# Transposing softmax probabilities on VectorE with block transposes and DMA in place of TensorE, and staggering the two attention units

## The chip, the cores and the metric

The kernel runs on one core of one Trainium2 chip. The metric is device time in microseconds (us) of one execution. Besides the execution times there is one profiled execution, read through several views: the summary page, groups of instructions by shape, the timeline of an engine, waits, the chain of work that ended last, and busy time in stretches. Engines are named as the profile names them: PE (TensorE matmuls), PEld (its weight loads), DVE (VectorE), ACT (ScalarE), POOL (GpSimd) and SP (the queue that issues most DMAs).

## The reference

Everything is float32. The input x has 4 batches of 512 rows of 1024 numbers; there are 16 heads of 64.

```
xn = layernorm(x)
q, k, v = xn @ Wq, xn @ Wk, xn @ Wv            # per head; rotary on q and k
p = softmax(causal(q @ k.T) / 8)               # 512 x 512 per head, lower triangle
s = (p @ v) @ Wo
r = softmax(xn @ gate_w.T)                     # 8 experts
f = ((xn * (r @ in_scale)) @ sign(weight).T) * (r @ out_scale) + bias
out = x + s * silu(f)
```

The change concerns the line of `p` and the product `p @ v`.

## The kernel before

The attention part runs over 16 groups, four to a batch. A group gives two units (`u0`, `u1`), and a unit is a pair of heads: its tiles hold head 0 in partitions 0 to 63 and head 1 in partitions 64 to 127 for q and k, or one head after the other in the free dimension for the probabilities. Query rows go in four tiles `i` of 128; tile `i` needs key columns 0 to 128(i+1) only, so a unit has 10 blocks (j, i) of 128 x 128 on or below the diagonal for each head.

The work of a unit, in the order of the code:

- `scores` (L517): for each query tile, one matmul per head into a PSUM tile. Then DVE adds the mask on the diagonal block (L528) and takes the row maximum (L532), ACT takes the exponential and the row sum (L535), DVE the reciprocal of the sum (L543), and POOL scales the probabilities (L545). `scores_1`, `scores_3` and `scores_02` do this for query tile 1, for tile 3, and for tiles 2 and 0, each time for both units of the group.
- `transpose_p` (L583): `p @ v` needs the probabilities with keys in partitions. TensorE transposes the 20 blocks of a unit through an identity matrix, four to a PSUM bank, and ACT (L589, three banks of five) or DVE (L587, two of five) copies the bank to an SBUF tile `pT`.
- `values` (L599): eight matmuls of v with the transposed blocks into one bank; DVE copies it over v's tile (L608), and SP stores that to DRAM (`at_d`, L609) for the output projection.

[...] Four are `ring`, used in turn by all projections, transposes and values; `ps_sc` is two tiles of two banks each for the scores, used also by `in_scales` and `out_scales` of the last batch.

TensorE's order is the order of the code, written by hand. While group k is projected (q, k and v, by a Strassen scheme of seven products for each pair of unit tiles: L342 for q and k, L429 for v), the attention of group k-1 is laid between the projection matmuls. One such stretch is called a slot: 84 projection matmuls (`fill`), spread evenly by `interleave` between the entries of a list `pieces`. A piece may be empty. A matmul in float32 shows as two instructions in the profile. For the other engines a planner orders the instructions by its own estimates of when their data is ready; `tc.keep_in_program_order` pins one behind whatever was written before it on its engine.

The list of a slot is five `transpose_p` banks of `w`, the scores of tile 1 and `values(w)`, five banks of `v`, the scores of tile 3 and `values(v)`, a wait, the scores of tiles 2 and 0, two waits. Here `w` and `v` are the two units of the group before; a unit's probabilities are thus transposed and used one slot after its scores. Into this list come the router's three steps at the first group of a batch, loads and layernorm of the next batch (`layernorm`, `transpose_x`), sign preparation (`make_sign`) in slots 5, 9, 12 and 13, and `in_scales` or `out_scales` in the last batch.

After slot 15 comes a tail written by hand: transposes, scores and values of what is left, between dense matmuls of the first FFN row pairs (`gated(0)`, `gated(1)`, L1003; one step of `dense` is four of these matmuls, just under a microsecond). Then follows the output projection with the rest of the FFN (L1242, L1182), which the change doesn't touch.

The DMAs of weights (`load_w`, L253 and L256: q or k weights, v weights) go through the same SP queue as the stores. The weight pool has three buffers of 1 MB.

Of the kernel before, what the change touches and what calls it, by code (L numbers as in the profile page):

```python
# [21 lines left out]
H, D = 16, 64  # L22
# [10 lines left out]
EPS = 1e-05  # L33
SCALE = 0.125


T_BANKS = [
    [(0, 0, i) for i in range(4)],
# [7 lines left out]
def t_place(h, j):  # L46

    return [(h, 0), (2 + h, 0), (4, 256 * h), (2 + h, 384)][j]
# [3 lines left out]
def attn_gated_ffn_kernel(  # L52
# [101 lines left out]
    def bank(name):  # L154
        return ring.tile([P, S], F32, tag="r", name=name)
# [349 lines left out]

    def probs(u, i):

        if i % 2:
            return PR[u, i]
        return PR[u, 0][:, :, P * i // 2 : P * i // 2 + (i + 1) * P]  # L510

    def scores(blocks):

        for u, i, ps in blocks:
            for h in range(2):
                r = h * D
                nc.tensor.matmul(  # L517
                    ps[:, h, :],
                    lhsT=Q[u][r : r + D, i * P : (i + 1) * P],
                    rhs=K[u][r : r + D, : (i + 1) * P],  # L520
                    start=True,
                    stop=True,
                )
        for u, i, ps in blocks:
            un = "%d_%d_%d" % u
            pt = probs(u, i)
            diag = ps[:, :, i * P : (i + 1) * P]
            nc.vector.tensor_tensor(  # L528
                diag, diag, mask[:, None, :].to_broadcast((P, 2, P)), op=ALU.add
            )  # L530
            nmx = st.tile([P, 2], F32, tag="nmx", name=f"nmx_{un}_{i}")
            nc.vector.tensor_reduce(nmx, ps, AX.X, ALU.max, negate=True)  # L532
            ssum = st.tile([P, 2], F32, tag="ssum", name=f"ssum_{un}_{i}")
            for h in range(2):
                nc.scalar.activation(  # L535
                    pt[:, h, :],
                    ps[:, h, :],
                    AF.Exp,
                    bias=nmx[:, h : h + 1],
                    accum_out=ssum[:, h : h + 1],  # L540
                )
# [8 lines left out]
    def sc_bank(u, n):  # L550
        return ps_sc.tile([P, 2, S], F32, tag="sc", name="sc_%d_%d_%d_%d" % (*u, n))

    def new_probs(u, n, cols, bufs):
        PR[u, n] = pp.tile(
            [P, 2, cols], F32, tag=f"p{n}", name="p%d_%d_%d_%d" % (n, *u), bufs=bufs
        )

    def scores_1(units):
        ps = sc_bank(units[0], 1)
        for u in units:  # L560
            new_probs(u, 1, 2 * P, 3)
        scores([(u, 1, ps[:, :, n * TH : (n + 1) * TH]) for n, u in enumerate(units)])

    def scores_3(units):
        for u in units:
            new_probs(u, 3, S, 2)
        scores([(u, 3, sc_bank(u, 3)) for u in units])

    def scores_02(units):
        blocks = []  # L570
        for u in units:
            new_probs(u, 0, S, 2)
            ps = sc_bank(u, 0)
            blocks += [(u, 2, ps[:, :, P:]), (u, 0, ps[:, :, :P])]
        scores(blocks)

    def transpose_p(u, n):
        un = "%d_%d_%d" % u
        if u not in PT:
            PT[u] = ptp.tile([P, 5, S], F32, tag="pT", name=f"pT_{un}")  # L580
        tp = tp_bank(f"ptp_{un}_{n}")
        for k, (h, j, i) in enumerate(T_BANKS[n]):
            nc.tensor.transpose(tp[:, k, :], probs(u, i)[:, h, j * P : (j + 1) * P], ident)  # L583
        dst = PT[u][:, n, :]
        src = tp.rearrange("p j q -> p (j q)")
        if n % 2:
            nc.vector.tensor_copy(dst, src)  # L587
        else:
            nc.scalar.copy(dst, src)  # L589

    def values(u):
        b, g, i = u
        pr = g + NGRP * i
        pv = bank("pv_%d_%d_%d" % u)
        for j in range(TPB):
            for h in range(2):
                r = h * D
                n, o = t_place(h, j)
                nc.tensor.matmul(  # L599
                    pv[r : r + D, j * P :],  # L600
                    lhsT=V[u][:, j, r : r + D],
                    rhs=PT[u][:, n, o : o + (TPB - j) * P],
                    start=(j == 0),
                    stop=(j == TPB - 1),
                )

        at = V[u].rearrange("p t c -> p (t c)")
        nc.vector.tensor_copy(at, pv)  # L608
        nc.sync.dma_start(  # L609
            out=at_d[b].rearrange("t p (c q) -> p t c q", c=NC)[:, :, pr, :],  # L610
            in_=at.rearrange("p (t q) -> p t q", t=TPB),
        )


# [224 lines left out]
    def attention_pieces(k, late):  # L839

        units = [(*groups[k], i) for i in range(2)]
        w, v = late

        def pt(u):
            return [lambda n=n: transpose_p(u, n) for n in range(5)] if u else []

        def with_values(scores_of, u):
            def both():
                scores_of(units)
                if u:  # L850
                    values(u)

            return both

        def wait():
            pass

        pieces = [
            *pt(w),
            with_values(scores_1, w),  # L860
            *pt(v),
            with_values(scores_3, v),
            wait,
            lambda: scores_02(units),
            wait,
            wait,
        ]
        return pieces, units

    def interleave(pieces, fill, n_fill):  # L870
# [8 lines left out]
    for k, (b, g) in enumerate(groups):  # L879
# [4 lines left out]
        if g == 0:  # L884
            routing = [lambda n=n: router(b, n) for n in range(3)]
            if k == 0:
                nothing = lambda: None
                pieces = [
                    routing[0],
                    lambda: (load_scales(in_scale), load_scales(out_scale)),  # L890
                    routing[1],
                    nothing,
                    routing[2],
                    lambda: split_scales(isc),
                    nothing,
                    nothing,
                    nothing,
                ]
            else:

                if b < B - 1:
                    pieces.insert(7, routing[0])
                pieces.insert(10, routing[1])
                pieces.insert(13, routing[2])
        elif g == 1 and b + 1 < B:

            pieces.insert(12, lambda: [load_x(b + 1, t) for t in range(2)])
            if b == 0:

                pieces.insert(1, lambda: split_scales(osc))  # L910
        elif g > 1 and b + 1 < B:
            t0 = 2 * (g - 2)
            for t in range(t0, t0 + 2):
                layernorm(b + 1, t)
            extra = [
                lambda t=t, h=h: transpose_x(b + 1, t, h) for t in range(t0, t0 + 2) for h in range(2)
            ]
            if g == 2:
                extra.append(lambda: [load_x(b + 1, t) for t in (2, 3)])

        step = max(1, (len(pieces) + len(extra)) // (len(extra) + 1))
        for n, e in enumerate(extra):
            pieces.insert(min(len(pieces), (n + 1) * step + n), e)
        if len(pieces) > 18:

            pieces.append(lambda: None)
        if k in (5, 9, 12, 13):
            n = {5: 0, 9: 2, 12: 4, 13: 6}[k]
            pieces.insert(8, lambda: make_sign(n + 1))
# [124 lines left out]
                if nxt:  # L1054
                    sum_wo(*nxt)

    for n in range(5):
        transpose_p(w, n)
    split(0, 0)
    scores_1(units)  # L1060
    split(0, 1)
    values(w)
    gates = gated(0)
    for ns in ((0, 1), (2, 3), (4,)):
        dense(gates, 2)
        for n in ns:
            transpose_p(v, n)
    scores_3(units)
    values(v)
    dense(gates, 6)  # L1070

    split(1, 0)
    out_scales(1, score_banks)
    dense(gates, 4)
    for _ in gates:
        pass
    split(1, 1)
    scores_02(units)
    gates = gated(1)
    dense(gates, 10)  # L1080
    for u in units:
        for ns in ((0, 1), (2, 3), (4,)):
            for n in ns:
                transpose_p(u, n)
            dense(gates, 1)
            if u == u1:
                sum_wo(2, ns[0] // 2)
        values(u)
    sum_wo(2, 3)
    for c in range(4):  # L1090
        sum_wo(4, c)
# [329 lines left out]
```

## Time and profile before

| what | value |
|---|---|
| time, median of 3 runs | 1165.63 us (1165.16 to 1165.71) |
| time of the profiled execution | 1165.57 us |
| its span, first to last instruction | 1163.7 us |
| busy PE / DVE / POOL / ACT | 1156.8 / 826.2 / 561.0 / 496.5 us |
| TensorE clock granted | 1.000 |
| DMA moved | 121.92 MB |

The span is cut in 40 slices of 29.1 us. The attention slots 1 to 15 lie between 75 and 825 us, the tail between 825 and 880 us, and the output projection with the FFN after that. "Busy" is the time in which at least one instruction of the engine was in progress. In groups of instructions, the number after the bar is busy time in us, then the mean duration of one in ns, then idle time of the engine just before them with what ended it. Durations of neighbours can overlap, so the distance between the starts of two instructions is the better price where the engine is full.

### The profile page before, as it was taken

How to read it: one execution, taken by the hardware profiler on the slowest of the kernel's cores; microseconds unless marked ns; L12 is line 12 of the kernel's file. 1: busy time of each engine (PE TensorE's matmuls, PEld its weight loads, DVE VectorE, ACT ScalarE, POOL GpSimd, SP SyncE). 2: the span in 40 equal slices, each digit the busy share in tenths (PEclk: the TensorE clock that was granted, in tenths of full speed). 3: DMA queues.
4: the chain of work that ended last, by engine and by line, in shares of the span. 5: the costliest groups of instructions: out<-in, count | busy, mean ns of one | idle time of the engine just before them, and what ended most of it. 6: DMA issues, size and time to landing. Idle time of an engine off the chain costs nothing.

```text
span 1163.7 us, 16130 instructions
## 1 busy us (share of the span) xinstructions
PE 1156.8 (99%) x5816; PEld 850.2 (73%) x5816; DVE 826.2 (71%) x1452; ACT 496.5 (43%) x1132; POOL 561.0 (48%) x590
## 2 busy tenths in 40 slices
PE   9999999999999999999999999999999999999998
PEld 8888787877878787877878787877775456545654
DVE  7886677568768667776867776675769786677664
ACT  2553673363366444535653563374442131223121
POOL 0681654264255435523743563364465554454535
PEclk9999999999999999999999999999999999999999
DMA  8413422222252142223236222220603324332331
GB/s 311 136 55 101 135 100 89 93 85 82 82 163 83 49 151 83 78 87 119 80 91 236 75 83 76 60 73 14 217 15 109 131 101 139 114 108 88 136 109 54
DMA packets 62319, 121.92 MB, mean 105 GB/s; under 512 B 5280, under 2 KB 40864, under 8 KB 56224
## 3 DMA queue, kind: packets, MB, share of 16 engines
q1 hardware_dynamic: 57376, 112.11, 28.8%
q0 software_dynamic: 4576, 8.39, 2.1%
q8 instruction: 46, 0.75, 0.3%
q10 hardware_dynamic: 288, 0.39, 0.1%
q14 instruction: 33, 0.27, 0.1%
HBM read 95.45 MB, written 25.43 MB: 104 GB/s over the span
## 4 chain that ended last, share of the span: by engine, by line
PE 97%; POOL 1%; issue 1%; ACT 1%; DVE 1%; POOLq 0%; DVEq 0%; ACTq 0%
PE pj L342 34%; PE pj L429 16%; PE wo L1242 16%; PE ff L1182 7%; PE sc L517 7%; PE pv L599 6%; PE ptp L583 6%; PE ff L1003 3%; PE xtp L210 1%; PE idle L793 1%; PE lg L622 1%; ACT p L535 0%; PE os L776 0%; PE is L746 0%; POOL uz L1270 0%
## 5 line engine op out<-in xcount | busy, mean ns | idle before, releaser
L545 POOL TENSOR_SCALAR p<-p,rs 128x128 f32<-128x128 f32 (+3 forms) x256 | 171.8, 684 | 261.6 <-DVE rs L543 261.5
L535 ACT ACTIVATE p<-sc,nmx 128x128 f32<-128x128 f32 (+3 forms) x256 | 132.5, 523 | 160.3 <-DVE nmx L532 153.7
L342 PE MATMUL pj<-X,w 128*128 128x256 f32 x576 | 138.3, 381 | 0.2 <-ACT X L216 0.2
L326 POOL TENSOR_TENSOR sw<-sw,sin_sb 128x512 f32<-128x512 f32 x64 | 87.8, 1371 | 91.8 <-ACT sw L324 76.1
L342 PE MATMUL pj<-T,S 128*128 128x256 f32 x512 | 123.3, 381 | 0.0
L342 PEld LDWEIGHTS pj<-X,w 128*128 128x128 f32 x576 | 105.1, 190 | 14.4 <-issue 1.8
L342 PE MATMUL pj<-T,w 128*128 128x256 f32 x448 | 107.6, 381 | 0.0
L589 ACT COPY pT<-ptp 128x512 f32<-128x512 f32 x96 | 56.1, 586 | 118.7 <-PE ptp L583 118.2
L532 DVE TENSOR_REDUCE nmx<-sc 128x2 f32<-128x512 f32 (+3 forms) x128 | 103.7, 820 | 2.8
L342 PEld LDWEIGHTS pj<-T,S 128*128 128x128 f32 x512 | 93.3, 190 | 12.7 <-issue 0.4
L429 PE MATMUL pj<-w,X 128*128 128x256 f32 x416 | 97.9, 381 | 0.0
L327 POOL TENSOR_TENSOR rot<-rot,sw 128x512 f32<-128x512 f32 x64 | 94.9, 1483 | 4.6
L583 PE MATMUL ptp<-ident,p 128*128 128x128 f32 x640 | 94.8, 273 | 0.3 <-ACT pT L589 0.3
L323 ACT ACTIVATE sw<-c 32x512 f32<-32x512 f32 x128 | 80.4, 628 | 32.1 <-DVE c L356 30.0
L583 PEld LDWEIGHTS ptp<-ident,p 128*128 128x128 f32 x640 | 79.0, 141 | 16.5 <-DVE pT L587 0.9
L342 PEld LDWEIGHTS pj<-T,w 128*128 128x128 f32 x448 | 82.1, 190 | 11.4 <-issue 1.8
L429 PEld LDWEIGHTS pj<-w,X 128*128 128x128 f32 x416 | 76.6, 190 | 10.5 <-issue 1.2
L517 PE MATMUL sc<-rot,rot 64*128 64x384 f32 (+3 forms) x512 | 82.0, 449 | 0.0
L429 PE MATMUL pj<-w,T 128*128 128x256 f32 x352 | 81.8, 383 | 0.0
L324 ACT ACTIVATE sw<-c 32x512 f32<-32x512 f32 x128 | 80.4, 628 | 1.7
L599 PE MATMUL pv<-pT,v 128*64 128x256 f32 (+3 forms) x512 | 76.0, 439 | 0.0
L528 DVE TENSOR_TENSOR sc<-sc,mask 128x256 f32<-128x256 f32 x128 | 53.8, 420 | 31.1 <-PE sc L517 30.8
(180 smaller groups left out, 2086.2 us busy)
## 6 DMA issues: line engine op xcount, KB each, us to landing
w<-in_wqk SPq DMA_DIRECT2D x31, 1024.0 KB, 5.6
w<-in_wv SPq DMA_DIRECT2D x16, 1024.0 KB, 4.8
x<-in_x SPq DMA_DIRECT2D x16, 512.0 KB, 3.7
xn_d<-X SPq DMA_DIRECT2D x16, 512.0 KB, 5.6
at_d<-v SPq DMA_DIRECT2D x32, 256.0 KB, 2.3
xp<-xn_d SPq DMA_DIRECT2D x16, 512.0 KB, 4.9
ap<-at_d SPq DMA_DIRECT2D x16, 512.0 KB, 4.8
xr<-in_x SPq DMA_DIRECT2D x32, 256.0 KB, 2.8
```

The source lines that it names most:

```text
L326: nc.gpsimd.tensor_tensor(sw, sw, sin_sb, op=ALU.mult)
L327: nc.gpsimd.tensor_tensor(rot, rot, sw, op=ALU.add)
L342: nc.tensor.matmul(ps, lhsT=wq[:, k, :], rhs=xq[:, k, :], start=(k == 0), stop=(k == 3))
L429: nc.tensor.matmul(ps[:, j, :], lhsT=xq[:, k, j * P : (j + 1) * P], rhs=wq[:, k, :], start=(k == 0), stop=(k == 3),)
L517: nc.tensor.matmul(ps[:, h, :], lhsT=Q[u][r : r + D, i * P : (i + 1) * P], rhs=K[u][r : r + D, : (i + 1) * P], start=True, stop=True,)
L532: nc.vector.tensor_reduce(nmx, ps, AX.X, ALU.max, negate=True)
L535: nc.scalar.activation(pt[:, h, :], ps[:, h, :], AF.Exp, bias=nmx[:, h : h + 1], accum_out=ssum[:, h : h + 1],)
L545: nc.gpsimd.tensor_scalar(pt[:, h, :], pt[:, h, :], rs[:, h : h + 1], 1.0, op0=ALU.mult, op1=ALU.mult,)
L583: nc.tensor.transpose(tp[:, k, :], probs(u, i)[:, h, j * P : (j + 1) * P], ident)
L599: nc.tensor.matmul(pv[r : r + D, j * P :], lhsT=V[u][:, j, r : r + D], rhs=PT[u][:, n, o : o + (TPB - j) * P], start=(j == 0), stop=(j == ...
L1182: nc.tensor.matmul(ps, lhsT=part[:, c, :], rhs=rhs[c // 2][:, (c % 2) * HALF : (c % 2 + 1) * HALF], start=(first and c == 0 and part is PA ...
L1242: nc.tensor.matmul(ps, lhsT=lhs[:, k, :], rhs=rhs[:, k, :], start=(first and k == 0), stop=(k == 3), skip_group_check=not first,)
```

## The change

A unit's probabilities now lie in one tile of 1280 columns per head (`PR[u]`; tile i begins at `QCOL[i]`). `scores(u)` issues all eight score matmuls of a unit together: tile 1 in two ring banks, one for each head, tile 3 in one `ps_sc` tile, tiles 2 and 0 in the other. `softmax(u, *tiles)` then does the mask, maximum, exponential, sum and scaling of the tiles it is given; for tile 1, mask and maximum are done for each head by itself.

`transpose_blocks(u)` takes the place of five `transpose_p` calls: ten DVE transposes, each of both heads' block (j, i), which transpose 32 x 32 pieces within each group of 32 partitions into a tile `y`; then 16 DMAs on SP that move 32 partitions by 640 columns each (80 KB) from `y` to the place of the piece within the transpose, over the unit's own probabilities. `values` reads the result with a stride of 640 columns, writes its bank in another order of columns, and ACT puts the order right while copying to v's tile.

The last unit of the last group keeps the TensorE path (`values(u1, blocks=False)`). The two units of a group stand half a slot apart: `u0` is scored at piece 4 and transposed at piece 10, its values come at piece 4 of the next slot; `u1` is scored at piece 12 and transposed at piece 2 of the next slot, its values come at piece 12 there. The router's steps, the second layernorm of a slot and the tail are moved to fit.

```diff
-    def scores(blocks):
+    def scores(u):
+        PR[u] = pp.tile([P, 2, 10 * P], F32, tag="p", name=f"p_{un}")
+        SC[u, 1] = [bank(f"sc_{un}_1_{h}")[:, :TH] for h in range(2)]
+        SC[u, 3], both = (
+            ps_sc.tile([P, 2, S], F32, tag="sc", name=f"sc_{un}_{n}") for n in (3, 0)
+        )
+        SC[u, 2], SC[u, 0] = both[:, :, P:], both[:, :, :P]
...
+        for i in (1, 3, 2, 0):
             for h in range(2):
...
+    def transpose_blocks(u):
+        y = ptp.tile([P, 20 * P], F32, tag="pT", name="y_%d_%d_%d" % u)
+        out = by_quarter(y).rearrange("p b (h n) -> p h b n", h=2)
+        for j in range(TPB):
+            for i in range(j, TPB):
+                src = probs(u, i)[:, :, j * P : (j + 1) * P]
+                o = OFF[j] + 32 * (i - j)
+                tc.keep_in_program_order(
+                    nc.vector.transpose(
+                        out[:, :, :, o : o + 32], src.rearrange("p h (b c) -> p h b c", b=4)
+                    )
+                )
+        PT[u] = by_quarter(PR[u].rearrange("p h n -> p (h n)"))
+        for n in range(4):
+            for a in range(4):
+                b = (a + n) % 4
+                nc.sync.dma_start(
+                    out=PT[u][32 * b : 32 * b + 32, a, :],
+                    in_=by_quarter(y)[32 * a : 32 * a + 32, b, :],
+                )
...
-        at = V[u].rearrange("p t c -> p (t c)")
-        nc.vector.tensor_copy(at, pv)
+        at = V[u]
+        if blocks:
+            nc.scalar.copy(
+                at.rearrange("p t (a q) -> p t a q", q=32),
+                pv.rearrange("p (a t q) -> p t a q", a=4, q=32),
+            )
...
-        pieces = [
-            *pt(w),
-            with_values(scores_1, w),
-            *pt(v),
-            with_values(scores_3, v),
-            wait,
-            lambda: scores_02(units),
-            wait,
-            wait,
-        ]
+        pieces = [nothing] * 16
+        if v:
+            pieces[2] = lambda: transpose_blocks(v)
+        pieces[4] = values_and_scores(w, u0)      # values(w), scores(u0), softmax(u0, 1, 3)
+        pieces[6] = lambda: softmax(u0, 2, 0)
+        pieces[10] = lambda: transpose_blocks(u0)
+        pieces[12] = values_and_scores(v, u1)
+        pieces[14] = lambda: softmax(u1, 2, 0)
...
                 if b < B - 1:
-                    pieces.insert(7, routing[0])
-                pieces.insert(10, routing[1])
-                pieces.insert(13, routing[2])
+                    pieces[5] = routing[0]
+                pieces[7], pieces[9] = routing[1:]
...
-            for t in range(t0, t0 + 2):
-                layernorm(b + 1, t)
+            layernorm(b + 1, t0)
+            pieces[8] = lambda: layernorm(b + 1, t0 + 1)
...
-    for n in range(5):
-        transpose_p(w, n)
     split(0, 0)
-    scores_1(units)
+    transpose_blocks(v)
+    values(w)
+    scores(u0)
+    softmax(u0, 1, 3)
     split(0, 1)
-    values(w)
     gates = gated(0)
...
+    dense(gates, 2)
+    softmax(u0, 2, 0)
     dense(gates, 6)
     split(1, 0)
     out_scales(1, score_banks)
-    dense(gates, 4)
+    dense(gates, 6)
+    values(v)
+    scores(u1)
+    softmax(u1, 1, 3)
+    transpose_blocks(u0)
...
```

More of the change, by code (lines that the diff above doesn't have):

```diff
@@ L34 @@
 SCALE = 0.125
+QCOL = [0, P, 3 * P, 6 * P]
+OFF = [0, 128, 256, 224]
 T_BANKS = [
@@ L506, in probs, with head @@
     def probs(u, i):
-        if i % 2:
-            return PR[u, i]
-        return PR[u, 0][:, :, P * i // 2 : P * i // 2 + (i + 1) * P]
-    def scores(blocks):
-        for u, i, ps in blocks:
+        return PR[u][:, :, QCOL[i] : QCOL[i] + (i + 1) * P]
+    SC = {}
+    def scores(u):
+        un = "%d_%d_%d" % u
+        PR[u] = pp.tile([P, 2, 10 * P], F32, tag="p", name=f"p_{un}")
[4 more added lines that the diff above has]
+        SC[u, 2], SC[u, 0] = both[:, :, P:], both[:, :, :P]
+        def head(i, h):
+            return SC[u, i][h] if i == 1 else SC[u, i][:, h, :]
+        for i in (1, 3, 2, 0):
             for h in range(2):
@@ L517, in scores @@
                 nc.tensor.matmul(
-                    ps[:, h, :],
+                    head(i, h),
                     lhsT=Q[u][r : r + D, i * P : (i + 1) * P],
@@ L523, in scores, with softmax @@
                 )
[L524 to L530, printed above, removed]
-            nmx = st.tile([P, 2], F32, tag="nmx", name=f"nmx_{un}_{i}")
-            nc.vector.tensor_reduce(nmx, ps, AX.X, ALU.max, negate=True)
+    def softmax(u, *tiles):
+        un = "%d_%d_%d" % u
+        for i in tiles:
+            pt, ps = probs(u, i), SC[u, i]
+            nmx = st.tile([P, 2], F32, tag="nmx", name=f"nmx_{un}_{i}")
+            at_once = [(ps[h][:, None, :], slice(h, h + 1)) for h in range(2)]
+            if i != 1:
+                at_once = [(ps, slice(0, 2))]
+                ps = [ps[:, h, :] for h in range(2)]
+            for v, hs in at_once:
+                diag = v[:, :, i * P : (i + 1) * P]
+                nc.vector.tensor_tensor(
+                    diag, diag, mask[:, None, :].to_broadcast((P, hs.stop - hs.start, P)), op=ALU.add
+                )
+                nc.vector.tensor_reduce(nmx[:, hs], v, AX.X, ALU.max, negate=True)
             ssum = st.tile([P, 2], F32, tag="ssum", name=f"ssum_{un}_{i}")
@@ L536, in scores @@
                     pt[:, h, :],
-                    ps[:, h, :],
+                    ps[h],
                     AF.Exp,
@@ L548, in scores, with by_quarter @@
                 )
[L550 to L575, printed above, removed]
+    def by_quarter(t):
+        return t.rearrange("p (a n) -> p a n", a=4)
+    def transpose_blocks(u):
[18 more added lines that the diff above has]
+                )
     def transpose_p(u, n):
@@ L579, in transpose_p @@
         if u not in PT:
-            PT[u] = ptp.tile([P, 5, S], F32, tag="pT", name=f"pT_{un}")
+            PT[u] = ptp.tile([P, 20 * P], F32, tag="pT", name=f"pT_{un}")
+            PT[u] = PT[u].rearrange("p (n q) -> p n q", q=S)
         tp = tp_bank(f"ptp_{un}_{n}")
@@ L589, in transpose_p, with values @@
             nc.scalar.copy(dst, src)
-    def values(u):
+    def values(u, blocks=True):
         b, g, i = u
@@ L594, in values @@
         pv = bank("pv_%d_%d_%d" % u)
+        by_block = by_quarter(pv)
         for j in range(TPB):
@@ L597, in values @@
                 r = h * D
[L598 to L604, printed above, removed]
-                )
-        at = V[u].rearrange("p t c -> p (t c)")
-        nc.vector.tensor_copy(at, pv)
+                if blocks:
+                    o = 320 * h + OFF[j]
+                    dst = by_block[r : r + D, :, 32 * j :]
+                    rhs = PT[u][:, :, o : o + 32 * (TPB - j)]
+                else:
+                    n, o = t_place(h, j)
+                    dst, rhs = pv[r : r + D, j * P :], PT[u][:, n, o : o + (TPB - j) * P]
+                nc.tensor.matmul(
+                    dst, lhsT=V[u][:, j, r : r + D], rhs=rhs, start=(j == 0), stop=(j == TPB - 1)
+                )
+        at = V[u]
+        if blocks:
+            nc.scalar.copy(
+                at.rearrange("p t (a q) -> p t a q", q=32),
+                pv.rearrange("p (a t q) -> p t a q", a=4, q=32),
+            )
+        else:
+            nc.vector.tensor_copy(at.rearrange("p t c -> p (t c)"), pv)
         nc.sync.dma_start(
-            out=at_d[b].rearrange("t p (c q) -> p t c q", c=NC)[:, :, pr, :],
-            in_=at.rearrange("p (t q) -> p t q", t=TPB),
+            out=at_d[b].rearrange("t p (c q) -> p t c q", c=NC)[:, :, pr, :], in_=at
         )
@@ L842, in attention_pieces, with nothing, values_and_scores @@
         w, v = late
-        def pt(u):
-            return [lambda n=n: transpose_p(u, n) for n in range(5)] if u else []
-        def with_values(scores_of, u):
+        u0, u1 = units
+        def nothing():
+            pass
+        def values_and_scores(before, u):
             def both():
-                scores_of(units)
-                if u:
-                    values(u)
-            return both
-        def wait():
-            pass
-        pieces = [
-            *pt(w),
-            with_values(scores_1, w),
-            *pt(v),
-            with_values(scores_3, v),
-            wait,
-            lambda: scores_02(units),
-            wait,
-            wait,
-        ]
+                if before:
+                    values(before)
+                scores(u)
+                softmax(u, 1, 3)
+            return both
+        pieces = [nothing] * 16
[6 more added lines that the diff above has]
+        pieces[14] = lambda: softmax(u1, 2, 0)
         return pieces, units
@@ L923, in attn_gated_ffn_kernel @@
             pieces.insert(min(len(pieces), (n + 1) * step + n), e)
-        if len(pieces) > 18:
-            pieces.append(lambda: None)
         if k in (5, 9, 12, 13):
@@ L1055, in dense @@
                     sum_wo(*nxt)
-    for n in range(5):
-        transpose_p(w, n)
     split(0, 0)
-    scores_1(units)
+    transpose_blocks(v)
+    values(w)
+    scores(u0)
+    softmax(u0, 1, 3)
     split(0, 1)
-    values(w)
     gates = gated(0)
[L1064 to L1069, printed above, removed]
+    dense(gates, 2)
+    softmax(u0, 2, 0)
     dense(gates, 6)
@@ L1077, in attn_gated_ffn_kernel @@
     split(1, 1)
-    scores_02(units)
     gates = gated(1)
+    dense(gates, 2)
+    softmax(u1, 2, 0)
     dense(gates, 10)
[L1081 to L1088, printed above, removed]
+    for ns in ((0, 1), (2, 3), (4,)):
+        for n in ns:
+            transpose_p(u1, n)
+        dense(gates, 1)
+        sum_wo(2, ns[0] // 2)
+    values(u0)
+    dense(gates, 1)
+    values(u1, blocks=False)
     sum_wo(2, 3)
```

## The prediction

> **What bounds the kernel now.** I read the page first: busy time and the chain of work that ended last.
>
> ```profile
> PE 1156.8 (99%) x5816; PEld 850.2 (73%) x5816; DVE 826.2 (71%) x1452; ACT 496.5 (43%) x1132; POOL 561.0 (48%) x590
> PEclk9999999999999999999999999999999999999999
> PE 97%; POOL 1%; issue 1%; ACT 1%; DVE 1%; POOLq 0%; DVEq 0%; ACTq 0%
> PE pj L342 34%; PE pj L429 16%; PE wo L1242 16%; PE ff L1182 7%; PE sc L517 7%; PE pv L599 6%; PE ptp L583 6%; PE ff L1003 3%; PE xtp L210 1%; PE idle L793 1%; PE lg L622 1%; ACT p L535 0%; PE os L776 0%; PE is L746 0%; POOL uz L1270 0%
> ```
>
> PE is never without work: the chain is PE for 97% of the span, at the full clock. So every TensorE instruction taken out shortens the kernel by its issue time, for as long as nobody else becomes late. The transposes (ptp) are 6% of that chain.
>
> Then PE's timeline inside a slot, for the price of a transpose.
>
> ```profile
> 416.84 0.60 PE L583 MATMUL ptp<-ident,p 128*128 128x128 f32 x4
> 417.28 1.46 PE L342 MATMUL pj<-T,S 128*128 128x256 f32 x6
> 418.57 0.59 PE L342 MATMUL pj<-T,w 128*128 128x256 f32 x2
> 419.00 0.60 PE L583 MATMUL ptp<-ident,p 128*128 128x128 f32 x4
> 419.44 1.89 PE L342 MATMUL pj<-T,w 128*128 128x256 f32 x8
> 421.26 1.13 PE L517 MATMUL sc<-rot,rot 64*128 64x256 f32 x8
> 422.33 1.94 PE L599 MATMUL pv<-pT,v 128*64 128x512 f32 x10
> ```
>
> Columns are start and length in us; lengths overlap, so starts count. Four transposes take 417.28 - 416.84 = 0.44 us of issue, 0.109 us each; eight projection instructions take 1.73 us (417.28 to 419.00), so one projection matmul (two instructions) is 0.43 us.
>
> Last, the busy time by stretch (PE, PEld, DVE, ACT, POOL; slots 1 to 15, the fullest 50 us I found for DVE, the tail) and the DVE rows that the change touches.
>
> ```profile
> 75.00:825.00 750.00, 750.00 (x4220) 596.29 (x4219) 525.64 (x1016) 374.07 (x889) 352.31 (x393) 1.00 0.29 94
> 475.00:525.00 50.00, 50.00 (x274) 39.55 (x273) 39.23 (x79) 21.11 (x53) 17.73 (x23) 1.00 0.28 96
> 825.00:880.00 55.00, 54.73 (x311) 39.98 (x311) 39.70 (x71) 22.88 (x63) 25.45 (x33) 1.00 0.28 99
> ```
> ```profile
> L528 DVE TENSOR_TENSOR sc<-sc,mask 128x256 f32<-128x256 f32 x128 | 53.8, 420 | 31.1 <-PE sc L517 30.8
> L587 DVE COPY pT<-ptp 128x512 f32<-128x512 f32 x64 | 43.6, 683 | 18.8 <-PE ptp L583 18.7
> L608 DVE COPY v<-pv 128x512 f32<-128x512 f32 x32 | 21.8, 680 | 11.7 <-PE pv L599 11.7
> ```
>
> DVE is the next busiest: 70% of the slots (525.64 of 750), 78% in the fullest 50 us. A slot is 750 / 15 = 50.0 us.
>
> **The change part by part.**
>
> PE transposes removed. All units but the last: 31 x 20 = 620. At 0.109 us that is 67.4 us (6% of the chain, 620 of 640, says the same). 560 of them lie in slots 2 to 15, 40 to a slot, 4.4 us each slot; 60 are in the tail, 6.5 us. All of it is on the path.
>
> DVE transposes added: 31 x 10 = 310, each of 2 x 128 = 256 elements for a partition. No row of before shows one. The nearest is L528, 256 elements in 0.42 us; neighbours overlap (L528 started at 390.93 us and the next DVE instruction at 391.26), so from below it is 0.33 us. From above: two copies of 128 x 128 (L665) at 0.282 make 0.56 us. [...] I take 0.42[...].
>
> [...] The trace's own row L583 has a mean of 273 ns, but starts 109 ns apart. [...] only the 109 ns are what PE gets back. [...] they ask 310 x 0.42 = 130 us of DVE for 67 us of PE. The case turns on whether DVE has that room.
>
> DVE's balance in slots 1 to 15. Added: 290 transposes (10 in slot 1, 20 in each later one) x 0.42 = 121.8. Removed: 28 units x 2 copies of L587 x 0.68 = 38.1, and 28 of L608 x 0.68 = 19.0. Tile 1's mask and maximum by head: one more mask (2 x 0.28 for 0.42) and one more maximum (2 x 0.42 for 0.69), 0.29 us for 30 units, 8.7. So 525.6 + 121.8 - 57.1 + 8.7 = 599 us. PE needs 750 - 61 = 689 us there. DVE comes to 87% (with 0.33: 83%[...]). PE stays the bound, with a nearer second.
>
> ACT loses three copies a unit (L589, 0.59 us) and gains one for pv: 62 us less in all. Moving the second layernorm away from the first may make ACT change tables between square root and exponential more often: the page of groups has 6 + 6 table loads of 1.28 us at L188 and L535; six more pairs are 15 us of ACT, which stands at 50%. Cost nothing; without cover 2.6 us in six slots. POOL's instructions stay (L545 is as before). That layernorm's DVE work (two statistics at 0.68, 0.20, 0.16, 0.85) is only moved within the slot, and DVE's sum stays. The router's DMAs (4 at 0.43 us, below) and the loads of x shift by some pieces in the same slot with tens of us to their readers: nothing.
>
> DMAs added: 16 a unit, 1.3 MB; 496 in all, 41 MB beside 121.92. SP's price comes from four in a row.
>
> ```profile
> 444.43 1.72 SPq L667 DMA_DIRECT2D rt_d<-rT  x4
> ```
>
> 0.43 us each: 16 take 6.9 us of SP, and these small ones land 2.0 us after issue (median of that row), so 9 us from the last transpose to complete data; two units a slot take 14 of 45 us of SP. A unit's chain after `transpose_blocks` is 4.2 us of DVE + 9 = 13 us. Its cover: from piece 10 to piece 4 of the next slot, and from piece 2 to piece 12, are 52 to 56 projection matmuls at 0.43 plus one group of scores and values, about 27 us. Behind these DMAs on SP queue the stores of `at_d`, weight loads and x. Weight loads have three buffers, so over ten us of slack; SP's longest wait for a weight buffer is 16.2 us (L253 on L342), in the order of the code it ends before the piece is reached. Cost nothing; if SP does hold the transposes for 14 us or more, PE waits at `values`.
>
> The transposes are pinned. They wait for POOL's scaling of tiles 2 and 0, given 20 projection matmuls (8.6 us) earlier; that chain is about 2.0 us of DVE, then ACT and POOL overlapping, 5 to 6 us in all, more when two rotary operations of POOL (L326, L327: 1.37 and 1.48) stand ahead. Then DVE holds, and everything behind it: the copies that empty ring banks. A bank is filled in 16 instructions, 3.5 us, so one such hold is mostly covered by the other banks.
>
> The score group is less covered. `scores(u)` takes two ring banks and `values` a third, so PE can go on after the half-filled projection bank only when pv or that bank has been emptied, while DVE has tile 1's and 3's masks and maxima (about 3 us) before it. PE's own scores take 2.4 us and the rest of the bank 0 to 3 us, so a wait is between nothing and about 1 us (emptying is 0.42 to 0.83 us). I take 0.5 us for each of 30 groups, 15 us. `in_scales` of slots 13 and 14 uses both score tiles two or three pieces ahead of `scores`, with DVE products of 4 x 0.68: 2 us each, 4. In the tail, `transpose_blocks(v)` comes right after the slot, and the last unit's `pT` needs `y` emptied by DMA: 2.5 us.
>
> The strided reads and writes of `values` have the same element counts: nothing from below; a tenth of L599's 6% of the span, 7 us, from above; I take 0.
>
> Sum, against the profiled execution's 1165.57 us (span 1163.7 and 1.9 around it; the median of the runs is 1165.63, the same): 1165.6 - 67.4 + 15 + 4 + 2.5 = 1119.7, say 1120.
>
> **The rivals.**
>
> A, nothing is lost: with 0.33 us a transpose and prompt emptying, 1165.6 - 67.4 = 1098, or 1100 with the tail. For it: PE waits for nobody today. Against it: DVE's idle time falls from 30% to 13 to 17%, and part of that is forced (DVE waits for ACT's exponential before L543 for 56.5 us in the slots).
>
> B, DVE becomes the bound of the slots: [...]
>
> C, slower: [...] The slots then take 525.6 - 57.1 + 8.7 + 56.5 = 533.7 plus 290 times its price, and reach today's 750 at 0.75 us. At 1.0 us they take 824: 1165.6 + 74 - 6.5 = 1233. [...] for it, only that no trace shows the operation, and that 1024 elements (L532) cost 1.22 us, were there four passes. That the data comes late through SP is a milder case: some us a unit, inside B.
>
> **How the numbers follow.** The likeliest case, PE bound with small waits, has 0.58 and a range of 1106 to 1132; A has 0.15, B 0.18, C 0.09. The range for 8 in 10 goes from 1097 to 1150: it leaves out C and the far end of B. A measurement of this kernel can tell about 0.2% (2.3 us) from no change. Faster: 0.58 + 0.15 + 0.18 less 0.03 for a B that eats all the gain, 0.88; the same 0.02; slower 0.10.
>
> **What would show it.** Right: PE busy near 1090 of a span near 1118; DVE near 900 us (826 + 130 - 63 + 9); transposes of 0.35 to 0.45 us; new PE waits of around 1 us for ring banks after the scores; PE hardly waiting for the DMAs. Wrong: transposes above 0.6 us with DVE at over 95% of the slots (B, C); PE or its weight loads waiting at L599's counterpart for the DMAs (SP late); PE waits of over 2 us a group; or projections stretched by late weights.

## The result and the profile after

The changed kernel takes 1160.93 us (median of 15 runs, 1157.75 to 1164.23) for 1165.38 before (15 runs, taken alongside): a ratio of 0.9962, 95% interval 0.9952 to 0.9972. Forecast were 1120 us and a range of 1097 to 1150: the direction was right, but nine tenths of the gain are missing.

The summary page of the changed kernel, its chain, and the busy time (PE, PEld, DVE, ACT, POOL, then granted clock, DMA share, GB/s) of slots and tail:

```profile
PE 1105.3 (95%) x5196; PEld 809.8 (70%) x5196; DVE 892.9 (77%) x1733; ACT 476.5 (41%) x1082; POOL 561.4 (48%) x590
PEclk9999999999989999998999999999999999999999
PE 39%; DVE 7%; issue 2%; ACT 2%; DMA 1%; SPq 1%; POOL 1%; POOLq 0%; DVEq 0%; ACTq 0%
```
```profile
75.00:825.00 750.00, 711.80 (x3712) 565.74 (x3711) 597.18 (x1309) 364.51 (x864) 358.15 (x401) 0.98 0.52 149
825.00:880.00 55.00, 47.45 (x213) 32.33 (x212) 39.62 (x67) 18.55 (x47) 27.14 (x29) 0.94 0.41 111
```

The 620 matmul instructions are gone (5816 to 5196), and DVE has what was reckoned for it. But PE is no longer always busy: 38 us of the slots and 7.5 us of the tail are idle, its clock is below 1.00 in both, and the chain runs through DVE, ACT, DMA and SP. The transposes themselves are as cheap as hoped:

```profile
L586 DVE STREAM_TRANSPOSE y<-p 128x256 f32<-128x256 f32 x310 | 108.2, 408 | 10.3 <-POOL p L568 10.1
```

Where the gain went is read by setting three marks of PE's timeline side by side: the end of the last projection, the first matmul of the output projection, and the end of the span (us).

| stage | before | after | saved | PE time of the transposes removed there |
|---|---|---|---|---|
| up to the last projection | 826.3 | 816.0 | 10.3 | 61.0 |
| tail | 54.1 | 58.1 | -3.9 | 6.5 |
| output projection and FFN | 283.3 | 285.1 | -1.8 | 0 |

So 50.7 us were lost in the slots and 10.4 in the tail. The 1.8 us of the last row are mostly one wait of 1.5 us for DVE at the start of the output projection (L1270), which is gone wherever the tail is mended (E7 to E10). PE's waits name the places (columns: total us, times, longest):

```profile
PE xtp L214 <- DVE x L200: 16.4, 6, 5.4
PE rt L696 <- DVE rex L692: 12.3, 3, 4.6
PE sc L532 <- DVE c L397: 3.8, 4, 1.3
PE ptp L608 <- ACT pT L614: 2.9, 1, 2.9
PE os L809 <- ACT p L558: 2.7, 1, 2.7
PE pv L631 <- issue: 2.6, 2, 1.3
PE ptp L608 <- POOL p L568: 1.9, 1, 1.9
```

The first two are not the new transposes. They are the transposes of the next batch's x, which wait for the layernorm that was moved to piece 8, and the router's third step, which waits for the second, now two pieces ahead of it. Six waits of 3.7 to 5.4 us are 27.8 of the 38.1 us. One of them on PE's timeline, and DVE's at the same time:

```profile
223.35 0.27 PE L666 MATMUL lt<-ident,lgs 128*128 128x128 f32 x1
226.49 1.89 PE L346 MATMUL pj<-T,w 128*128 128x256 f32 x8
232.09 0.33 PE L696 MATMUL rt<-ident,rex 128*128 128x128 f32 x1 [3.71 <-DVE rex L692]
232.22 3.58 PE L346 MATMUL pj<-T,w 128*128 128x256 f32 x8
```
```profile
226.10 0.42 DVE L360 TENSOR_TENSOR c<-pj,part 128x256 f32<-128x256 f32 x1 [2.34 <-ACT part L366]
227.96 1.28 DVE L300 TENSOR_TENSOR S<-w 128x512 f32<-128x512 f32 x1
229.17 1.25 DVE L680 TENSOR_TENSOR rex<-rex,rrs 128x32 f32<-128x32 f32 x1
230.34 0.68 DVE L300 TENSOR_TENSOR w<-w 128x512 f32<-128x512 f32 x1
```

The router's ten small operations of DVE stand in one queue with weight sums, and PE, whose order is fixed, waits at L696. It is the order of this queue more than its fullness. The router's second step leaves PE at 223.62 us (L666), but DVE, which has to begin with its result, first stands idle for 2.34 us behind an addition (L360) that waits for ACT's copy. Then L300 and L680 take 1.28 and 1.25 us; the next L300 takes 0.68, and L680 in slot 12 takes 0.18. Why these two are slow here was not tested.

After the wait eight instructions take 3.58 us where the same eight took 1.89 us before it: PE runs at a lower clock (the granted clock of these 5 us, 0.72, is shown at E4). The gaps explain 38.1 of the 50.7 us; the other 12.6 were put down to this clock, for the experiments to test.

### The profile page after: what moved, and what is told of

Same layout as the page of the kernel before. It is cut to its first block, busy times and chain, and to the rows that moved or that the text cites. A ratio compares the mean times of both kernels' runs of the same rounds, so it can differ in the third digit from the quotient of the medians.

```text
span 1159.2 us, 16044 instructions
## 1 busy us (share of the span) xinstructions
PE 1105.3 (95%) x5196; PEld 809.8 (70%) x5196; DVE 892.9 (77%) x1733; ACT 476.5 (41%) x1082; POOL 561.4 (48%) x590
## 4 chain that ended last, share of the span: by engine, by line
PE 39%; DVE 7%; issue 2%; ACT 2%; DMA 1%; SPq 1%; POOL 1%; POOLq 0%; DVEq 0%; ACTq 0%
PE wo L1270 14%; PE pj L346 8%; PE ff L1210 7%; PE pj L433 5%; PE pv L631 2%; PE sc L532 2%; PE ff L1030 1%; DVE y L586 1%; SPq L596 1%; ACT p L558 1%; DMA xn_d<-X 1%; DVE nmx L555 1%; DVE S L300 0%; ACT sw L327 0%; DVE w L300 0%
## 5 line engine op out<-in xcount | busy, mean ns | idle before, releaser
L568 POOL TENSOR_SCALAR p<-p,rs 128x256 f32<-128x256 f32 (+3 forms) x256 | 173.4, 691 | 221.4 <-DVE rs L566 186.8
L558 ACT ACTIVATE p<-sc,nmx 128x256 f32<-128x256 f32 (+3 forms) x256 | 132.9, 525 | 102.3 <-DVE nmx L555 75.6
L346 PE MATMUL pj<-X,w 128*128 128x256 f32 x576 | 132.8, 381 | 0.2 <-ACT X L220 0.2
L586 DVE STREAM_TRANSPOSE y<-p 128x256 f32<-128x256 f32 x310 | 108.2, 408 | 10.3 <-POOL p L568 10.1
L555 DVE TENSOR_REDUCE nmx<-sc 128x1 f32<-128x256 f32 (+3 forms) x160 | 109.7, 688 | 4.3
L346 PEld LDWEIGHTS pj<-T,w 128*128 128x128 f32 x448 | 89.6, 203 | 13.9
L433 PE MATMUL pj<-w,X 128*128 128x256 f32 x416 | 94.5, 380 | 0.0
L532 PE MATMUL sc<-rot,rot 64*128 64x384 f32 (+3 forms) x512 | 83.3, 444 | 5.1 <-DVE c L397 3.8
L433 PEld LDWEIGHTS pj<-w,X 128*128 128x128 f32 x416 | 78.2, 190 | 11.2 <-issue 0.8
L552 DVE TENSOR_TENSOR sc<-sc,mask 128x256 f32<-128x256 f32 (+1 forms) x160 | 58.2, 366 | 34.5 <-PE sc L532 34.3
L433 PE MATMUL pj<-w,T 128*128 128x256 f32 x352 | 79.8, 381 | 0.6 <-DVE v L459 0.6
L532 PEld LDWEIGHTS sc<-rot,rot 64*128 64x128 f32 x512 | 51.6, 186 | 36.7 <-issue 18.4
L631 PE MATMUL pv<-p,v 128*64 128x512 f32 (+1 forms) x496 | 73.6, 439 | 2.6 <-issue 2.6
L433 PEld LDWEIGHTS pj<-w,T 128*128 128x128 f32 x352 | 66.1, 190 | 10.1 <-issue 0.8
```

What stands on the lines that cost most here:

```text
L346: nc.tensor.matmul(ps, lhsT=wq[:, k, :], rhs=xq[:, k, :], start=(k == 0), stop=(k == 3))
L433: nc.tensor.matmul(ps[:, j, :], lhsT=xq[:, k, j * P : (j + 1) * P], rhs=wq[:, k, :], start=(k == 0), stop=(k == 3),)
L532: nc.tensor.matmul(head(i, h), lhsT=Q[u][r : r + D, i * P : (i + 1) * P], rhs=K[u][r : r + D, : (i + 1) * P], start=True, stop=True,)
L555: nc.vector.tensor_reduce(nmx[:, hs], v, AX.X, ALU.max, negate=True)
L558: nc.scalar.activation(pt[:, h, :], ps[h], AF.Exp, bias=nmx[:, h : h + 1], accum_out=ssum[:, h : h + 1],)
L568: nc.gpsimd.tensor_scalar(pt[:, h, :], pt[:, h, :], rs[:, h : h + 1], 1.0, op0=ALU.mult, op1=ALU.mult,)
```

## The experiments

Theory: PE stands still where work was moved close to its reader, and is clocked down after each long wait. Rival: DVE is simply fuller, and PE would wait at some other place. All ratios are to the kernel before, with 95% intervals; the clock is that of the profiled run.

**E1: the layernorm moved back.**

```diff
-            pieces[8] = lambda: layernorm(b + 1, t0 + 1)
+            layernorm(b + 1, t0 + 1)
```

> The changed kernel with one edit undone: both layernorms of a slot again at its start. Theory (PE stands still where work was moved close to its reader, and is then clocked down): the three waits of PE for the normalized rows in slots 2, 6 and 10 (5.0, 5.4, 5.1 us in the changed kernel) go, and with each some 2 us of lowered clock; 1161 - 22 = 1139 us, granted clock from 0.984 to about 0.992. Rival (DVE is simply fuller, 80% of the slots instead of 70%, and PE would wait at some other place): the same work of DVE only moves, the time stays within 5 us of 1161.

Measured: 1150.43 us, 0.9878 (0.9861 to 0.9894), clock 0.988. The three waits are gone, half of the forecast gain is there. The other half is missing because about 6 us of new gaps came, the longest of 3.2 and 2.8 us ahead of score matmuls (L532), where PE waits for a ring bank, and the clock rose less than forecast. Both sides are partly right.

**E2: the router's third step further from the second.**

```diff
-                pieces[7], pieces[9] = routing[1:]
+                pieces[7], pieces[13] = routing[1:]
```

> The changed kernel with the third step of the router put at piece 13 instead of 9, six pieces after the second step instead of two. Theory: PE's three waits for the router's probabilities in slots 4, 8 and 12 (3.7, 4.1, 4.6 us) go, with some 2 us of lowered clock each; 1161 - 18 = 1143 us. Rival (DVE fuller): within 5 us of 1161.

Measured: 1151.54 us, 0.9888 (0.9873 to 0.9903), clock 0.989. The same picture: its three waits are gone, half of the gain arrives, and a gap of 2.7 us appears ahead of L532 in the slot of the third router.

**E3: both edits.**

> The changed kernel with both edits: layernorms at the start of the slot, the router's third step at piece 13. Theory: the two gains add, 1161 - 40 = 1121 us, granted clock above 0.99 in the slots, DVE's busy time unchanged near 893 us. Rival (DVE fuller): PE's waits come back at other places, 1150 us or more.

Measured: 1140.92 us, 0.9792 (0.9777 to 0.9806), clock 0.986. The two single gains add (10.5 and 9.4 to 20.0), so the theory names a true cause; but 20 us short of the forecast, and the rival's gaps at other places are there too. The eight ahead of the scores (L532) all wait for DVE to empty a ring bank; one of the longest, on PE's timeline and DVE's:

```profile
158.83 5.14 PE L532 MATMUL sc<-rot,rot 64*128 64x256 f32 x16 [3.21 <-DVE part L360]
```
```profile
154.70 1.42 DVE L586 STREAM_TRANSPOSE y<-p 128x256 f32<-128x256 f32 x4
156.04 0.38 DVE L360 TENSOR_TENSOR part<-pj,part 128x256 f32<-128x256 f32 x1
156.35 1.99 DVE L300 TENSOR_TENSOR S<-w,w 128x1024 f32<-128x1024 f32 x1
158.27 0.41 DVE L360 TENSOR_TENSOR part<-pj,part 128x256 f32<-128x256 f32 x1
```

`scores` asks first for two ring banks (tile 1). DVE has to empty a projection bank with two additions (L360), and block transposes and a weight sum stand ahead of and between them; PE starts when the second one is done. Such gaps ahead of L532 come to 14.7 us in E3's slots.

**E4: the waits filled with idle work.** The dependencies of the changed kernel stay; PE only isn't still while it waits.

```diff
-                pieces[7], pieces[9] = routing[1:]
+                pieces[7] = routing[1]
+                pieces[9] = lambda: (keep_warm(40), routing[2]())
...
+            if g == 2:
+                extra[2] = lambda: (keep_warm(48), transpose_x(b + 1, t0 + 1, 0))
```

> The changed kernel with idle transposes of the identity put before the six long waits (48 before the third transpose of x in slots 2, 6 and 10, 40 before the router's third step): PE is busy with nothing while it waits, the dependencies stay. Theory: the waits remain as busy time, but the clock stays at 1.000 there; only the clock's part of the loss returns, 12 us, so 1149 us. Rival (the lowered clock has nothing to do with the waits): clock still 0.984, 1161 us; in the router's groups of slots 0 the 40 are not wanted and cost up to 0.7 us each.

Measured: 1149.42 us, 0.9867 (0.9853 to 0.9882), clock 0.996. Busy time in two stretches of 5 us, first of the changed kernel, then of E4 (the clock is the third number from the end):

```profile
230.00:235.00 5.00, 2.91 (x8) 2.40 (x9) 3.03 (x11) 0.00 (x0) 0.36 (x1) 0.72 0.03 7
330.00:335.00 5.00, 1.55 (x6) 1.46 (x7) 3.53 (x7) 0.93 (x2) 2.77 (x2) 0.62 0.00 0
```
```profile
230.00:235.00 5.00, 5.00 (x28) 4.46 (x26) 3.12 (x9) 0.37 (x1) 0.72 (x1) 1.00 0.28 74
330.00:335.00 5.00, 4.90 (x25) 4.42 (x26) 4.48 (x13) 0.37 (x1) 0.29 (x1) 1.00 0.06 12
```

With 264 idle transposes more, the kernel is 11.5 us faster, as the 12 us of clock said. That the waits lower the clock is thus shown, and its price is measured. After the one of 5.1 us at 540 us of the changed kernel the granted clock of the next 5 us is 0.50. Shorter waits lowered it in some places and not in others (last section). The prediction had no such term.

**E5: the same moves in the kernel before.** TensorE transposes stay; only the second layernorm of a slot is put close ahead of its reader, and the router's third step one piece nearer to the second.

```diff
-                pieces.insert(13, routing[2])
+                pieces.insert(12, routing[2])
...
-            for t in range(t0, t0 + 2):
-                layernorm(b + 1, t)
+            layernorm(b + 1, t0)
...
+        if g > 1 and b + 1 < B:
+            third = pieces.index(extra[2])
+            pieces.insert(third - 1, lambda: layernorm(b + 1, t0 + 1))
```

> The kernel before, TensorE transposes and all, with the second layernorm of a slot put one piece ahead of the transposes of x that read it (some 4 projection matmuls, 1.7 us, as in the changed kernel), and the router's third step one piece nearer to the second. Theory (the distance to the reader makes the wait, not DVE's fullness): PE waits 3 to 5 us in slots 2, 6 and 10 and is clocked down after it, 1165 + 15 to 20 = about 1182 us, clock about 0.99. Rival (DVE at 70% would hide it, only the fuller DVE of the change made it late): within 5 us of 1165.

Measured: 1176.50 us, 1.0095 (1.0080 to 1.0110), clock 0.998. The waits appear without any block transpose:

```profile
PE xtp L210 <- DVE x L196: 8.1, 4, 2.8
PE rt L663 <- DVE rex L659: 0.9, 1, 0.9
```
```profile
231.88 0.27 PE L633 MATMUL lt<-ident,lgs 128*128 128x128 f32 x1
236.36 0.30 PE L663 MATMUL rt<-ident,rex 128*128 128x128 f32 x1
```

But they are 2.5 to 2.8 us long, not 5, and the distance isn't the one that was meant. The edit puts the layernorm two of this slot's 23 pieces ahead of its reader, which is seven projection matmuls and a bank of transposes, about 3.5 us; in the changed kernel it is one of 21 pieces, four matmuls, 1.7 us. The longer distance alone accounts for 1.7 of the 2.6 us by which the waits differ (an estimate). So for the layernorm the distance is shown as a cause, and that the fuller DVE adds to it is not.

For the router E5 shows the opposite. Its third step is due 4.2 to 4.5 us after the second here (slot 4 is in the last two lines above; eight or nine matmuls and a bank of transposes), nearer than in the changed kernel (5.0 to 6.3 us), and yet PE waits 0, 0 and 0.9 us for it, not 3.7, 4.1 and 4.6. More distance cures that wait (E2), but nearness alone doesn't make it: what stands in DVE's queue in the changed kernel does.

**E6: the banks of tile 1 asked for last.** On top of E3.

```diff
-        SC[u, 1] = [bank(f"sc_{un}_1_{h}")[:, :TH] for h in range(2)]
-        for i in (1, 3, 2, 0):
+        for i in (3, 2, 0, 1):
+            if i == 1:
+                SC[u, 1] = [bank(f"sc_{un}_1_{h}")[:, :TH] for h in range(2)]
...
-                softmax(u, 1, 3)
+                softmax(u, 3, 1)
```

> E3 (both edits) with the score matmuls of a unit in the order 3, 2, 0, 1 and the softmax in the order 3, 1: the two ring banks of tile 1 are asked for last, 1.8 us later. Theory (the rest of the loss in the slots is PE waiting for ring banks that DVE has not emptied, 15 us of gaps ahead of L532, and the clock after them): most of these gaps shrink by up to 1.8 us, 1141 - 12 = about 1129 us, clock to 0.99. Rival (the banks are as late at the next projection, DVE being behind): the gaps move from L532 to L346 and L433, time within 4 us of 1141.

Measured: 1128.81 us, 0.9685 (0.9671 to 0.9700), clock 0.993. The gaps ahead of the scores shrink from 14.7 us to 0.7, and 12 us are gained as forecast. But most of the gaps move, as the rival said: 2.1, 2.1, 1.7 and 1.4 us stand ahead of L433 now, others of 0.7 to 1.5 us elsewhere. All gaps of PE in the slots add up to 21.1 us in E3 and to 16.7 in E6, 4.4 less, while the slots end 13.1 us earlier. The other 8.7 us are put down to the clock: none of E6's gaps in the slots is longer than 2.1 us, where four of E3's had 2.6 to 3.2, and the mean granted clock of 75 to 825 us rises from 0.98 to 0.99. PE's waits for ring banks were the next cause, by their length more than by their sum.

Three of the gaps ahead of L433 (5.6 us in all) end with ACT's exponentials (L559): those of tile 1, which empty the ring banks, come behind those of tile 3, and a change of ACT's tables can stand ahead of both (in E3 one of 1.28 us at 161.28 us).

**E7: the tail mended.** On top of E3: `out_scales` three steps of `dense` later, and u0 of the last group by `transpose_p` as in the kernel before.

```diff
+    dense(gates, 3)
     out_scales(1, score_banks)
-    dense(gates, 6)
+    dense(gates, 3)
     values(v)
...
-    transpose_blocks(u0)
...
-    dense(gates, 10)
+    dense(gates, 8)
+    for u in units:          # transpose_p, dense and values as in the kernel before
```

> E3 with the tail mended: out_scales three steps of dense later, and u0 of the last group transposed by TensorE too (20 transposes, 2.2 us of PE), so that nothing in the tail waits for the DMAs of u0. Theory: the tail's three gaps (2.7, 1.8, 3.0 us) and the lowered clock after them, some 10 us, shrink to 2; less 2.2 us for the transposes: 1141 - 6 = 1135 us. Rival (the tail is held by DVE and POOL, not by these two): within 2 us of 1141.

Measured: 1132.67 us, 0.9721 (0.9698 to 0.9745), clock 0.995. The three gaps of the tail are gone; one of 3.2 us is left, where `values(v)` waits for v's DMAs. The tail was held where the theory said.

**E8: E6 and E7 together.**

> E3 with both further edits (scores of tile 1 last, tail mended). Theory: the gains add, about 1123 us, clock above 0.99. Rival: as in the two single runs, 1135 us or more.

Measured: 1122.14 us, 0.9630 (0.9614 to 0.9646), clock 0.996. Still a wait of 3.3 us at `values(v)` of the tail. Its 16 DMAs took 14.6 us of SP, right behind eight loads of wo.

**E9: v of the tail by TensorE.** On top of E8: no `transpose_blocks(v)`, but five `transpose_p(v, n)` between three steps of `dense` after `out_scales`, and `values(v, blocks=False)`.

> E8 with v of the last group transposed by TensorE in the tail (20 transposes, 2.2 us of PE), so that no unit in the tail waits for DMAs. Theory (PE's wait of 3.3 us at values(v) is for the 16 DMAs, which stand among the loads of wo): the wait and the clock after it, some 4 us, go for 2.2 us of PE and two copies of DVE: 1122 - 2 = 1120 us. Rival: no change or slower by up to 2 us, where DVE's copies in the tail are late.

Measured: 1125.29 us, 0.9657 (0.9644 to 0.9670), clock 0.993. A miss: the wait for DMAs is gone, but PE waits 2.4 us for the copy of a bank by DVE (`pT`, L613), which stands behind other work, and the median is 3.2 us above E8's. That is the rival's reason, and more than its 2 us: in this order DVE comes to that copy too late.

**E10: the transposes of v ahead of the loads of wo.** On top of E8.

```diff
+    transpose_blocks(late[1])
     bias_sb = vec.tile([P, E], F32, name="bias_sb")
...
     split(0, 0)
-    transpose_blocks(v)
     values(w)
```

> E8 with transpose_blocks(v) of the tail written ahead of the loads of bias and wo, so that its 16 DMAs are issued before those 4.5 MB. Theory (the 16 DMAs took 14.6 us of SP because the DMA engines were full of wo): they take about 7 us, PE does not wait at values(v), 1122 - 4 = 1118 us. Rival (SP or DVE then hold the loads of wo, at and bias, and a later reader waits): 1122 us or more.

Measured: 1118.11 us, 0.9595 (0.9582 to 0.9609), the best version. SP's timeline in E10 at that place, the first line for v's DMAs:

```profile
788.45 10.01 SPq L597 DMA_DIRECT2D p<-y  x16
798.51 2.50 SPq L1001 DMA_DIRECT2D wo<-in_wo  x5
```

The 16 DMAs take 10.0 us instead of 14.6 and PE doesn't wait for them; five of the eight loads of wo come after, without a reader that waits. They do not take the 7 us that I expected: 10.0 us is what 16 of them take elsewhere too. E10's page and its slots up to 775 us:

```profile
PE 1090.6 (98%) x5216; PEld 793.7 (71%) x5216; DVE 882.6 (79%) x1726; ACT 458.9 (41%) x1072; POOL 561.8 (50%) x590
75.00:775.00 700.00, 680.81 (x3615) 536.30 (x3615) 573.07 (x1267) 336.52 (x823) 348.97 (x389) 1.00 0.53 152
```

DVE is at 82% there (573.07 of 700), more than in the changed kernel's slots, and the clock is whole. The last projection ends at 784.2 us, 42.1 earlier than before; PE's remaining gaps in the slots add up to 19.2 us; together 61.3 for the 61.0 us that the transposes took. The tail takes 48.9 us, 5.3 less than before. So this account of the slots closes: what is still missing there is all in gaps that the timeline shows.

## Why the prediction was right or wrong

Right, by its own steps:

- The price of a PE transpose, 0.109 us by starts and not by durations. E10's account returns it in full. That the block transposes ask more of DVE (108.2 us busy) than they give back to PE (67.4 us) did not decide: DVE had the room.
- The price of a block transpose: 0.42 us taken, 0.408 measured, and ten in a row take 3.38 us (0.34 each). DVE's slots were put at 599 us and have 597; its total at 900 and is 893. Rivals B and C, whose dearer transposes no trace had shown, fall.
- The strided reads and writes of `values` cost nothing: these matmuls have a mean of 439 ns before and after.

Right in size only, by luck:

- The ring banks at the scores: 15 us were taken for 30 groups, for PE waiting after the scores while DVE is at masks and maxima. The changed kernel has 5.0 us of gaps ahead of L532. With the moved work put back (E3) they add up to 14.7 us, but as eight gaps of 0.8 to 3.2 us, and ahead of the scores, where DVE empties a projection bank late between block transposes and weight sums. Their effect on the clock was not reckoned.

Wrong:

- The step that failed is the cost of what was moved, put at nothing. Of the layernorm it said that its DVE work "is only moved within the slot", of the router that its DMAs and the loads shift "with tens of us to their readers". Both looked at sums and at DMAs, not at the chain to the nearest reader on PE. The third transpose of x stands four projection matmuls (1.7 us) after piece 8; the chain of statistics, square root with a change of ACT's tables (1.28 us at 122.77 us of the changed kernel) and normalization took PE 5.0 us of waiting there. The router's steps stand about eleven matmuls apart in slots 4 and 8, and PE waited 3.7 and 4.1 us, with DVE beginning the chain late (in E5, at less distance, it doesn't wait at all in these two slots). Undone, these two bring 20 us (E3).
- A term was missing: the clock after a wait. E4 measures 11.5 us for the six waits, two fifths as much as the waits themselves (27.8).
- The tail's 2.5 us were 10.4. `out_scales` moved nearer to the exponentials that read its banks (2.7 us), and the last unit's `pT` waited for `y`, whose 16 DMAs in turn waited. E7, E8 and E10 bring this back.
- `in_scales` was put at 4 us in slots 13 and 14: the changed kernel has three gaps in slot 13, of 0.4 to 1.3 us, and none in slot 14, and all three are waits for additions at L397 and L459.
- A DMA of 80 KB costs SP 0.59 us (median), not the 0.43 of a 16 KB one. In the slots the cover was wide enough; in the tail, behind wo, it was not.
- Two slips without weight for the sum: ACT loses 62 copies, about 36 us, and not 62 us (busy 496.5 before, 476.5 after, with twelve more changes of tables for 15.4 us); and before, SP waits up to 22.3 us at a weight load (L253 on L455), more than the 16.2 given as the longest.

With all these places mended the change gives 1118 us, close to the 1120 of the sum. That the two agree is partly luck: the sum had no clock and no moved work in it, and E10 has other orders than the change.

Open: how much of E6's gaps ahead of L433 the change of tables makes was not tested; 1.28 of 2.08 us is an estimate from its length. The 1.3 to 1.5 us ahead of L632, which the profile puts down to issue, fit a ring bank: such a wait ends 0.1 us after DVE emptied a bank in the changed kernel (1.28 us ahead of 186.17 us, L218) and in E3 (2.64 us ahead of 558.45 us, L360). No run tests it. For the router, the order of DVE's queue and the slow L300 and L680 were read from the trace and not changed one by one.

## What to carry to other kernels

Price a moved step by the distance to its nearest reader on the engine with the fixed order, and by what stands before it in the queue where it lands, not by whether the engine that runs it has room; the same chain of ten small operations kept PE waiting for 3.7 us in one order of that queue and not at all in another. A saving on the busiest engine is only collected in full if that engine is never left waiting for some microseconds, since a long wait can be paid a second time in clock (E4: 11.5 us for six waits of 3.7 to 5.4 us). The sorted list of its waits shows such places; the sums of busy time didn't. When an engine gets fuller, ask for scarce buffers as late as the order allows (E6: 12 us).

## What the runs showed of the hardware

Whether a wait lowers the clock isn't fixed by its length alone. The six of 3.7 to 5.4 us all did in the changed kernel: in the 5 us after each the granted clock was 0.50 to 0.71. But E6 and E10 have the same wait of 2.08 us at the same matmul; after it 20 instructions take 6.27 us in E6 and 4.58 us in E10:

```profile
164.43 6.27 PE L433 MATMUL pj<-w,X 128*128 128x256 f32 x20 [2.08 <-ACT p L559]
```
```profile
165.54 4.58 PE L433 MATMUL pj<-w,X 128*128 128x256 f32 x20 [2.08 <-ACT p L559]
```

The clock granted in the 5 us from 165 us is 0.66 in E6 and 1.00 in E10. A wait of 1.55 us at 263 us of E3 was followed by 0.73. So these runs give no single length that parts the waits that lower the clock from those that don't. It also fits that the changed kernel's own runs spread by 6.5 us where those of the kernel before spread by 1.5: the two longest have a mean clock of 0.980, the eight shortest 0.984 to 0.986.
